# A two-layer block on one core: four of a block's sixteen pair adds given to GpSimd

## The chip, the core and the metric

The kernel runs on one core of a Trainium2 chip. The core has a matrix engine (TensorE, "PE" in the profile, with its weight loads as "PEld"), three elementwise engines (VectorE "DVE", ScalarE "ACT", GpSimd "POOL") and a queue engine for transfers (SyncE "SP"). Each engine works through its own instructions in program order, and engines wait for one another through semaphores. The metric is the device time of one execution in microseconds. Before the change, three runs gave 5608.47, 5620.06 and 5624.56 us; the median is 5620.06.

## What is computed

The reference is two transformer-like layers on x of shape (4, 1024, 256), float32. The first has a recurrence over time and a mixture of experts. The second, which the change touches, has a pairwise attention and a dense feed-forward network:

```python
q = einsum('bnc,ac->bna', X, Wq)          # a = 64
k = einsum('bnc,ac->bna', X, Wk)
Vy = einsum('bnc,dc->bnd', X, Wy_w) + Wy_b
e = relu(rho_signed_sqrt(q[:, :, None, :] + k[:, None, :, :]))
scores = einsum('bija,a->bij', e, Wphi)
ex = exp(scores - max(scores, axis=-1))
denom = sum(ex, axis=-1)
part1 = einsum('bij,bjc->bic', ex, Vy)
Ew = einsum('bij,bija->bia', ex, e)
part2 = einsum('bia,ca->bic', Ew, We_w) + We_b * denom
return (part1 + part2) / (denom + EPS_DEN)
```

For every query i, key j and channel a, q + k is formed, cut at zero, its root is taken (with 1e-8 under it), weighted with Wphi and summed over a for the scores, and weighted with ex and summed over j for Ew. That is 4 x 1024 x 1024 x 64 elements.

## The kernel before

`first_layer` (L143) does the first layer, `pair_attention` (L801) the second one, with the last part of the first layer and the dense network (`dense`, L1196) woven into it.

In the attention a `Block` is 32 queries of one batch; there are 128. It is worked in 8 **pairs**, numbered p from 0 to 7. A pair is one tile `s` of 128 partitions x 2 x 1024 float32. A partition holds one of 16 queries and one of 8 channels; the two **halves** (h = 0 and 1) are two groups of channels, and pairs 0 to 3 and 4 to 7 are the two sets of 16 queries. The keys lie ready in SBUF, repeated over partitions (`kB`), and the queries are a column per partition (`qt`). `Block.pair` (L1305) makes a pair:

- an **add** for each half: key plus query, cut at zero. On ScalarE this is an activation with the query as its bias (L1313), on VectorE a two-step instruction with scalar operands, add and maximum (L1315). The tuple `RELU_ON_SCALAR` (L35) lists by 2p + h which halves ScalarE takes: 0, 2, 4, 8, 10, 12, that is half 0 of pairs 0, 1, 2, 4, 5 and 6. VectorE makes the other ten;
- a **square root** over both halves on ScalarE, in place (L1316);
- the **score matmuls** on TensorE, 8 for each half (L1320), summed over the block in the PSUM tile `sc`.

When a block's scores are there, `top` (L1328) takes the maximum of a row on VectorE (L1330, L1332) with a small matmul (L1333), `exps` (L1335) takes its negative on VectorE (L1337) and the exponentials on ScalarE (L1339), for which ScalarE loads another table, and `spread` (L1342) repeats them over partitions with matmuls into the PSUM tile `xb` (L1345). `turn` and `turned` (L1348 to L1357) transpose them. Then `weigh` (L1359) multiplies each half with `xb` on VectorE, in place, and sums over keys into a column of `ew` (L1364, two instructions in the profile for each half).

The order is written out by hand, and every engine keeps it. The loop from L1463 goes through the blocks and their pairs: weigh pair p of this block; at p = 5 `top` of the next block, at p = 6 its `exps` and first `spread`; then `work(ROOM[p])` (L1429), which issues some of the waiting dense, finishing and preparing steps, with a budget for each p; then `make()` (L1443), which makes the pair that lies 12 ahead (11 in the first blocks). So after the weigh of pair p, pair p + 4 of the next block is made for p up to 3, and pair p - 4 of the block after for p from 4. The tiles `s` come from a ring of 12 buffers (L31): the pair just made uses the buffer that the weigh before it gives free.

A dense step's matmuls go into one of two PSUM banks; two steps later VectorE empties it (L1238, L1213, L1207, L1277). `finish` (L1368) ends four blocks: VectorE computes `fin` (L1410), GpSimd adds it to the input (L1412) and SP stores that (L1413). GpSimd's only other regular work in this stage is the sum at L1278 at the end of a dense tile, also stored by SP. GpSimd issues no transfers here. `prepare` (L918) makes keys, queries and values of the next batch, with transfers on SP (L955, L980).

Of the kernel before, what the change touches and what calls it, by code (L numbers as in the profile page):

```python
# [9 lines left out]
ALU = mybir.AluOpType  # L10
# [21 lines left out]
PREP = 12  # L32
ROOM = (3, 5, 6, 6, 6, 3, 2, 6)
LATE = 2
RELU_ON_SCALAR = (0, 2, 4, 8, 10, 12)  # L35

CONSTS = {"ident": P, "tri": P, "ones": P, "avg": P, "center": P, "heads": P, "gather": P, "rank": NE, "same": P, "pick": 8 * P, "part": 4, "query": 16, "row0": P}
CH_MX, CH_MW, CH_MK, CH_MV, CH_MR, CH_MG, CH_TD, CH_U, CH_LW, CH_LB = range(10)
# [763 lines left out]
def pair_attention(tc, a, link, out, cols_of, seen, ident, eps):  # L802
# [10 lines left out]
    nc = tc.nc  # L813
# [4 lines left out]
    with tc.tile_pool(name="at_w", bufs=1) as wp, tc.tile_pool(name="at_2", bufs=2) as p2, tc.tile_pool(  # L818
# [24 lines left out]
        for i in range(2):  # L843
            t = wp.tile([P, 4, P], F32, tag=f"ewt{i}", name=f"ewt{i}")
            nc.gpsimd.memset(t, 0.0)
            ewt.append(t)
            t = wp.tile([P, 4, 64], F32, tag=f"ew{i}", name=f"ew{i}")
# [34 lines left out]
        kB = {}  # L882
# [415 lines left out]
        class Block:  # L1298
# [6 lines left out]
            def pair(self, p):  # L1305
                t = ring.tile([P, 2, T], F32, tag="s", name="s")
                self.s[p] = t
                s = p // 4
                for h in range(2):
                    g = (2 * p + h) % 8  # L1310
                    q = qtab[self.b][:, 2 * (self.n % NB) + s, g : g + 1]
                    if 2 * p + h in RELU_ON_SCALAR:
                        nc.scalar.activation(t[:, h, :], kB[self.b][g], AF.Relu, bias=q)  # L1313
                    else:
                        nc.vector.tensor_scalar(t[:, h, :], kB[self.b][g], q, 0.0, ALU.add, ALU.max)  # L1315
                nc.scalar.activation(t, t, AF.Sqrt, bias=eps_rho)  # L1316
                for h in range(2):
                    g = (2 * p + h) % 8
                    for j in range(4):
                        nc.tensor.matmul(  # L1320
                            self.sc[32 * j : 32 * j + 32, 0:256],
                            wsel[:, g, 16 * (1 - s) : 16 * (1 - s) + 32],
                            t[:, h, 256 * j : 256 * (j + 1)],
                            start=p == 0 and h == 0,
                            stop=p == 7 and h == 1,
                        )
# [264 lines left out]
```

## Time and profile before

| | us |
|---|---|
| median of 3 runs | 5620.06 (5608.47 to 5624.56) |
| the profiled execution | 5612.39 |
| its span, first to last instruction | 5610.4 |
| first layer and start of the attention | 0 to about 1270 |
| pair attention with dense work | about 1270 to 5390 |
| dense work alone | about 5390 to 5610 |

| busy us, whole span | TensorE | weight loads | VectorE | ScalarE | GpSimd |
|---|---|---|---|---|---|
| | 4574.4 | 2695.6 | 4532.2 | 3854.0 | 534.3 |

TensorE's mean granted clock was 0.884 of full speed. A row of the groups reads: source line, engine, operation, what it writes and what it reads with their shapes, count, then busy time and the mean duration in ns of one, then the idle time of the engine just before these instructions and what ended most of it. A row in the order of time reads: start in us, length in us, engine, line, operation, tiles, number of instructions, and in brackets the idle time before and what ended it. Durations of neighbours on an engine overlap at the ends, so their spacing is somewhat less than their length. The chain of work is followed back from the last instruction, at each step to what released it or to the instruction before it on its engine.

### The profile page before, as it was taken

The numbers are of one execution on the slowest core, as the hardware profiler recorded it, in microseconds if no ns is written. First come the engines' busy times: TensorE is split into PE (matmuls) and PEld (weight loads), VectorE is DVE, ScalarE is ACT, GpSimd is POOL, SyncE is SP. The second block draws the span as 40 slices with busy tenths as digits, with TensorE's granted clock in tenths as the row PEclk, the third lists the DMA queues.
The fourth block names the chain that finished last, engine by engine and source line by source line (L and its number), as shares of the span: only waits on it lengthen the run. The fifth ranks groups of instructions, "written<-read, shape, count | busy, mean of one in ns | idle before, by whom it ended". The sixth has DMA issues, their size and how long they took to land.

```text
span 5610.4 us, 74442 instructions
## 1 busy us (share of the span) xinstructions
PE 4574.4 (82%) x28714; PEld 2695.6 (48%) x28714; DVE 4532.2 (81%) x7889; ACT 3854.0 (69%) x3550; POOL 534.3 (10%) x463
## 2 busy tenths in 40 slices
PE   6789888765778778888896788897888897888888
PEld 2233333332345445555463555564555564555566
DVE  5777777656888888889988788888889989898951
ACT  2322222117888888888887888888788888888840
POOL 3434433220000000000000000000000000000000
PEclk8789999886889889998898889898899898988999
DMA  4333333332011131211112221111211211111123
GB/s 133 100 94 94 95 89 97 102 95 68 25 36 47 38 70 61 82 61 57 45 69 46 60 82 59 51 63 34 71 53 60 87 65 44 57 56 50 44 95 115
DMA packets 223734, 385.48 MB, mean 69 GB/s; under 512 B 69346, under 2 KB 114963, under 8 KB 222995
## 3 DMA queue, kind: packets, MB, share of 16 engines
q1 hardware_dynamic: 211890, 378.46, 21.7%
q8 instruction: 226, 3.70, 0.3%
q10 hardware_dynamic: 11488, 2.25, 0.2%
q14 instruction: 130, 1.06, 0.1%
HBM read 340.74 MB, written 39.86 MB: 68 GB/s over the span
## 4 chain that ended last, share of the span: by engine, by line
PE 44%; DVE 31%; ACT 16%; SPq 4%; issue 3%; DMA 2%; POOL 0%; ACTq 0%; DVEq 0%; POOLq 0%
PE ff_ps L1249 14%; DVE s L1364 13%; PE sc L1320 8%; ACT s L1316 7%; DVE s L1315 5%; PE e_ps L591 5%; PE xb L1345 4%; DVE state L777 2%; ACT s L1313 2%; PE ff_ps L1226 2%; PE out_ps L1268 2%; ACT wide L1290 2%; ACT L1316 2%; DVE pr L779 2%; SPq L955 1%
## 5 line engine op out<-in xcount | busy, mean ns | idle before, releaser
L1364 DVE CUSTOM_DVE_ANT_0 s<-s,xb 128x1024 f32<-128x1024 f32 x2048 | 2412.6, 1215 | 37.7 <-PE xb L1345 36.5
L1316 ACT ACTIVATE s<-s,eps 128x2048 f32<-128x2048 f32 x1024 | 2039.0, 2001 | 379.3 <-DVE s L1315 362.3
L1320 PE MATMUL sc<-s,wsel 128*32 128x256 f32 x16384 | 1235.4, 427 | 727.2 <-ACT s L1316 725.8
L1320 PEld LDWEIGHTS sc<-s,wsel 128*32 128x32 f32 x16384 | 463.3, 117 | 1334.5 <-ACT s L1316 898.6
L1249 PE MATMUL ff_ps<-wide,fw 128*128 128x256 f32 x4096 | 983.5, 389 | 8.6 <-ACT wide L1290 8.5
L1315 DVE TENSOR_SCALAR s<-kB,qt 128x1024 f32<-128x1024 f32 x1280 | 947.3, 758 | 35.3 <-DMA wk<-in_Wk_dram 17.1
L1313 ACT ACTIVATE s<-kB,qt 128x1024 f32<-128x1024 f32 x768 | 875.0, 1139 | 102.7 <-DMA wk<-in_Wk_dram 59.1
L1249 PEld LDWEIGHTS ff_ps<-wide,fw 128*128 128x128 f32 x4096 | 769.2, 193 | 181.9 <-issue 74.5
L1345 PE MATMUL xb<-ex,pick 128*128 128x256 f32 x2048 | 591.6, 439 | 16.6 <-ACT ex L1339 15.8
L1345 PEld LDWEIGHTS xb<-ex,pick 128*128 128x128 f32 x2048 | 423.3, 218 | 208.1 <-issue 75.5
L591 PE MATMUL e_ps<-wd,hid 128*128 128x512 f32 x896 | 424.7, 621 | 0.0
L709 POOL TENSOR_TENSOR kv<-vb,out_k 128x512 f32<-128x512 f32 x256 | 323.7, 1272 | 332.4 <-DVE state L777 202.7
L777 DVE TENSOR_TENSOR_SCAN state<-dec,carry,kv 128x512 f32<-128x512 f32 x256 | 326.0, 1273 | 9.6 <-POOL carry L772 5.0
L1412 POOL TENSOR_TENSOR xr<-xr,fin 128x256 f32<-128x256 f32 x32 | 34.2, 1068 | 2877.8 <-DVE fin L1410 2650.4
L591 PEld LDWEIGHTS e_ps<-wd,hid 128*128 128x128 f32 x896 | 174.8, 201 | 245.0 <-issue 238.4
L779 DVE TENSOR_TENSOR pr<-state,rec 128x512 f32<-128x512 f32 x256 | 176.0, 687 | 110.8 <-ACT state L775 57.5
L1226 PE MATMUL ff_ps<-wide,fw 128*128 128x256 f32 x1024 | 255.5, 400 | 3.3 <-DVE wide L1213 1.5
L1238 DVE TENSOR_TENSOR wide<-ff_ps,ffn_s 128x512 f32<-128x512 f32 x128 | 88.1, 688 | 208.7 <-PE ff_ps L1249 207.7
L769 ACT COPY carry<-state 128x1 f32<-128x1 f32 x255 | 47.8, 188 | 271.4 <-DVE state L777 270.3
L1226 PEld LDWEIGHTS ff_ps<-wide,fw 128*128 128x128 f32 x1024 | 200.2, 201 | 50.1 <-issue 12.1
L1330 DVE TENSOR_REDUCE own<-sc 128x1 f32<-128x256 f32 x128 | 54.0, 422 | 170.6 <-PE sc L1320 170.6
L1364 DVE DVE_READ_ACCUMULATOR2_ANT ew<- 128x1 f32 x2048 | 168.7, 82 | 0.0
(247 smaller groups left out, 3879.9 us busy)
## 6 DMA issues: line engine op xcount, KB each, us to landing
fw<-in_ffw_dram SPq DMA_DIRECT2D x352, 512.0 KB
vb<-vd SPq DMA_DIRECT2D x1024, 64.0 KB
wd<-in_w_down_dram SPq DMA_DIRECT2D x28, 1024.0 KB
kB<-kd SPq DMA_DIRECT2D x32, 512.0 KB
kd<-wide SPq DMA_DIRECT2D x24, 512.0 KB
vd<-out_v SPq DMA_DIRECT2D x8, 512.0 KB
kd<-kn SPq DMA_DIRECT2D x16, 256.0 KB
vy<-vd SPq DMA_DIRECT2D x4, 1024.0 KB
```

Source lines behind the costliest of these rows:

```text
L591: nc.tensor.matmul(ps, hid[:, k, t * P : (t + 1) * P], wd[:, k, :], start=k == 0, stop=k == HID // P - 1)
L709: nc.gpsimd.tensor_mul(kv, vb[:, g % 2, :], ready[u]["k"][:, n // HN, :])
L777: nc.vector.tensor_tensor_scan(s[:, 1 : U + 1], dec, kv, c, ALU.mult, ALU.add)
L779: nc.vector.tensor_mul(pr, s[:, 0:U], rec)
L1226: nc.tensor.matmul(ps[:, h, :], w[:, k, o : o + P], hT[:, k, :], start=k == 0, stop=k == 1)
L1249: nc.tensor.matmul(ps[:, h, :], w[:, k * P : (k + 1) * P], of[:, k, :], start=k == 0, stop=k == 7)
L1313: nc.scalar.activation(t[:, h, :], kB[self.b][g], AF.Relu, bias=q)
L1315: nc.vector.tensor_scalar(t[:, h, :], kB[self.b][g], q, 0.0, ALU.add, ALU.max)
L1316: nc.scalar.activation(t, t, AF.Sqrt, bias=eps_rho)
L1320: nc.tensor.matmul(self.sc[32 * j : 32 * j + 32, 0:256], wsel[:, g, 16 * (1 - s) : 16 * (1 - s) + 32], t[:, h, 256 * j : 256 * (j + 1)], s ...
L1345: nc.tensor.matmul(xb[:, 256 * j : 256 * (j + 1)], pick[:, j, s, :], self.ex, start=True, stop=True)
L1364: nc.vector.tensor_tensor_reduce(t[:, h, :], t[:, h, :], self.xb[s], 1.0, 0.0, ALU.mult, ALU.add, ew[:, self.n % 4, col : col + 1])
```

## The change

GpSimd takes four of a block's adds, `ADD_ON_POOL`: half 1 of pairs 0, 2, 4 and 6. ScalarE's list becomes half 0 of pairs 0, 1, 3, 5 and 7. VectorE keeps seven: half 1 of pairs 1, 3, 5 and 7 and half 0 of pairs 2, 4 and 6. The two halves of a pair are now issued with half 1 first, so that GpSimd's add stands before the other engine's in the program.

```diff
-RELU_ON_SCALAR = (0, 2, 4, 8, 10, 12)
+RELU_ON_SCALAR = (0, 2, 6, 10, 14)
+ADD_ON_POOL = (1, 5, 9, 13)
...
                 s = p // 4
-                for h in range(2):
+                for h in (1, 0):
                     g = (2 * p + h) % 8
                     q = qtab[self.b][:, 2 * (self.n % NB) + s, g : g + 1]
-                    if 2 * p + h in RELU_ON_SCALAR:
+                    if 2 * p + h in ADD_ON_POOL:
+                        nc.gpsimd.tensor_scalar(t[:, h, :], kB[self.b][g], q, 0.0, ALU.add, ALU.max)
+                    elif 2 * p + h in RELU_ON_SCALAR:
                         nc.scalar.activation(t[:, h, :], kB[self.b][g], AF.Relu, bias=q)
                     else:
                         nc.vector.tensor_scalar(t[:, h, :], kB[self.b][g], q, 0.0, ALU.add, ALU.max)
```

## The prediction

> **What bounds the kernel now.** I read the busy times first, then one stretch of the second layer, then the chain of work that ended last, then the groups, and last the order of time around single instructions.
>
> ```profile
> PE 4574.4 (82%) x28714; PEld 2695.6 (48%) x28714; DVE 4532.2 (81%) x7889; ACT 3854.0 (69%) x3550; POOL 534.3 (10%) x463
> 4650.00:5150.00 500.00, 425.65 (x3204) 274.13 (x3197) 448.86 (x792) 439.07 (x324) 7.71 (x6) 0.90 0.15 52
> PE 44%; DVE 31%; ACT 16%; SPq 4%; issue 3%; DMA 2%; POOL 0%; ACTq 0%; DVEq 0%; POOLq 0%
> ```
>
> The second line is a stretch inside the pair attention (TensorE, weight loads, VectorE, ScalarE, GpSimd). VectorE is busy 90% of it, ScalarE 88%, TensorE 85%, GpSimd under 2%. So three engines are nearly full and coupled, and none is the bound alone; the third line, the chain's shares, says the same. An edit there is worth its count on the chain, not its busy time.
>
> ```profile
> L1364 DVE CUSTOM_DVE_ANT_0 s<-s,xb 128x1024 f32<-128x1024 f32 x2048 | 2412.6, 1215 | 37.7 <-PE xb L1345 36.5
> L1316 ACT ACTIVATE s<-s,eps 128x2048 f32<-128x2048 f32 x1024 | 2039.0, 2001 | 379.3 <-DVE s L1315 362.3
> L1315 DVE TENSOR_SCALAR s<-kB,qt 128x1024 f32<-128x1024 f32 x1280 | 947.3, 758 | 35.3 <-DMA wk<-in_Wk_dram 17.1
> L1313 ACT ACTIVATE s<-kB,qt 128x1024 f32<-128x1024 f32 x768 | 875.0, 1139 | 102.7 <-DMA wk<-in_Wk_dram 59.1
> L410 POOL TENSOR_TENSOR rk<-out_r,out_k 128x1024 f32<-128x1024 f32 x8 | 18.8, 2348 | 3.1 <-ACT out_r L403 3.1
> L845 POOL MEMSET ewt<- 128x512 f32 x2 | 1.1, 526 | 1.9 <-DMA x<-x 1.9
> ```
>
> Durations overlap at their ends, so I cost by the spacing of starts in the order of time: an add on VectorE 0.67 us, a weigh 1.14 (two with what follows: 2.40), a square root on ScalarE 1.91, an add there 1.17. A pair with one add on each engine takes VectorE 3.07 and ScalarE 3.08 us.
>
> From 1650 to 5376 us (115 of 128 blocks) I went through the chain in order of time and gave each add and square root the pair it belongs to, by its running number. Square roots on the chain: pair 1 61 times, pair 2 62, pair 7 14, pair 6 11, the others 3 to 7. 49 times the chain goes from VectorE's add of pair 1 into its square root, on through the exponentials on ScalarE, and out by pair 2's add and square root to TensorE. VectorE's adds on it: pair 0 69, pair 7 first half 54, pair 3 first half 25; the second halves of pairs 2, 4, 6: 25, 29, 35. ScalarE's: pair 2 62, pair 6 12, pair 4 3.
>
> **The change, part by part.** Of a block's adds, half 1 of pairs 0, 2, 4, 6 goes from VectorE to GpSimd; half 0 of pairs 2, 4, 6 goes from ScalarE to VectorE; half 0 of pairs 3 and 7 from VectorE to ScalarE. No DMA, tile or matmul changes.
>
> *Saved on ScalarE:* pair 2's add leaves a run in which ScalarE alone is on the chain: 62 x 1.14 = 71 us; pairs 4 and 6: 15 x 1.14 = 17; the new adds lengthen pairs 3 and 7, whose square roots are on the chain 5 + 14 times: 19 x 1.14 = 22 lost. Net 66.
>
> *Saved on VectorE:* pairs 3 and 7: 79 x 0.67 = 53. Pair 0 would be 69 x 0.67 = 46, but behind 49 of these ScalarE has a path almost as long: from the end of the weigh, 0.04 + 1.17 + 1.91 + 1.17 = 4.29 us to pair 1's square root, against VectorE's 0.67 + 2.40 + 0.60 (the row maximum) + 0.75 = 4.42. So 49 x 0.13 + 20 x 0.67 = 19. Pairs 2, 4, 6 swap one add for another: 0. **Saved in all: 66 + 53 + 19 = 138 us.**
>
> *The length of the GpSimd add* is not in the trace. Its product of two tensors takes 0.73 us for 256 elements, 1.27 for 512 and 2.35 for 1024 (2.1 ns an element), its memset of 512 0.53 (0.84 ns an element between 256 and 512; 0.96 us for 1024 as an estimate). An add with one tensor input lies between. The Trainium skill ("GPSIMD Engine Reference", section 4.1 Engine selection) says not to put elementwise work there, and calls one-input operations roughly line-rate; its section 3.1 gives a best loop of about 1.8 cycles an element at 1.2 GHz. The estimates by it are 1.05 and 1.7 us with the 0.18 us of start that the trace's rows leave. I take **1.65**, the middle of the trace's two rows, and keep 1.0 to 2.35, and more if its loop is poor.
>
> *The port.* Here a rule speaks against the change:
>
> ```profile
> 1915.28 1.28 POOL L1278 TENSOR_TENSOR res<-res,wide 128x512 f32<-128x512 f32 x1 [42.86 <-DVE wide L1277]
> 2250.67 2.42 DVE L1315 TENSOR_SCALAR s<-kB,qt 128x1024 f32<-128x1024 f32 x2
> 2250.98 1.57 POOL L1278 TENSOR_TENSOR res<-res,wide 128x512 f32<-128x512 f32 x1 [109.61 <-issue]
> 3035.32 0.74 DVE L1315 TENSOR_SCALAR s<-kB,qt 128x1024 f32<-128x1024 f32 x1
> 3035.49 1.17 POOL L1412 TENSOR_TENSOR xr<-xr,fin 128x256 f32<-128x256 f32 x1 [59.75 <-DVE fin L1410]
> 3035.98 1.21 DVE L1364 CUSTOM_DVE_ANT_0 s<-s,xb 128x1024 f32<-128x1024 f32 x1
> ```
>
> Two VectorE adds take 1.41 us alone; with a GpSimd sum started inside the first they take 2.42. The sum waited for the first add and the second add waited 1.01 us for the sum, whose own length is 1.28. The weigh (one operand in PSUM) runs beside GpSimd unhurt. The Trainium skill ("SBUF — State Buffer", Who interferes with whom) says that whoever issues first holds the shared pair for the whole instruction. By the rule a VectorE add behind a 1.65 us add waits up to 1.65, by the row 1.65 - 0.27 = 1.38; I use the row. Who is first?
>
> ```profile
> 4698.25 0.08 DVE L1364 DVE_READ_ACCUMULATOR2_ANT ew<- 128x1 f32 x1
> 4698.37 1.15 ACT L1313 ACTIVATE s<-kB,qt 128x1024 f32<-128x1024 f32 x1 [0.28 <-DVE ew L1364]
> 4698.37 0.75 DVE L1315 TENSOR_SCALAR s<-kB,qt 128x1024 f32<-128x1024 f32 x1
> ```
>
> The ring has 12 buffers and runs 12 ahead, so a pair's adds wait for the weigh just issued. VectorE's add starts 0.04 us after it, ScalarE's too; GpSimd starts 0.08 to 0.09 us after the VectorE result it waits for (L1410 ends at 3035.40, L1412 starts at 3035.49). So being earlier in the program does not help GpSimd: I take VectorE first, by 0.04 us. Of the 345 adds of pairs 2, 4, 6, 230 follow the weigh at once; in 29 GpSimd is held by the sum of L1412 anyway; in 86 other VectorE work stands between and GpSimd gets the port. Summed over their gaps, that stalls VectorE 31 us (10 for an add of 1.25 us, 81 for 2.35).
>
> *The new wait.* A square root of pair 2, 4 or 6 can start 0.04 + 0.67 + 1.65 + 0.04 = 2.40 us after the weigh, that of pair 0 (no VectorE add) at 1.77; now both start at 1.22 where ScalarE has no backlog. Behind it on ScalarE are the next pair's add, exponentials and copies; on TensorE its score matmuls, and behind those the dense layers. Pair 2 is free of it: its square root starts no earlier than 3.95 now. Costs on the chain: pair 0 before the 49 crossings, 49 x 0.55 = 27; pairs 4 and 6, 14 x 1.2 = 17; the backlog that pair 6 hands through pair 7 to pair 0, 0.65 us at about half of the 49, 16; the port, 31 us at the share of adds on the chain (0.35), 11; the row maximum and the weigh, which wait for TensorE 32 and 43 times now, about 0.4 us later each, 30. **Cost: 101 us.** On GpSimd's queue a block adds 4 x 1.65 = 6.6 us to an engine idle 98% here; the sums of L1412 and L1278, and their stores on SP's queue, come at most one add later.
>
> **Sum.** -138 + 101 = -37 us in 115 blocks, x 128/115 = -41. The profiled execution took 5612.4 us (span 5610.4, 2.0 around it): 5571. It lies 7.7 under the median of the runs, 5620.1: **5580 us**, 0.7% less. The last 221 us, dense layers alone, and the first layer stay.
>
> **The rivals.** *A short GpSimd add, 1.05 us:* the costs fall to 0 + 8 + 3 + 1 + 10 = 22, net -116 x 1.11 = -129: **5490**. For it the memset row; against it the two-tensor row. Were the three adds a block saved in full, 384 x 0.67 = 257, it would be 5363, but VectorE is under a third of the chain.
>
> *GpSimd gets the port first (slower):* at the 230 adds that follow the weigh at once VectorE waits 1.38 + 0.04 = 1.42, 327 us; 89 of 345 of them are on the chain, 84 us, less 10 as those square roots come earlier: -37 + 84 - 10 = +37, x 1.11 = 41: **5661**. It decides when the claim comes under 0.04 us after the weigh. Against it the 0.08 us; for it that both are tens of nanoseconds.
>
> *A long GpSimd add, 2.35 us:* 61 + 27 + 16 + 28 + 60 = 192, less 138 = +54, x 1.11 = 60: **5680**; at 3 us some 5780. Between 1.65 and 2.35 the balance turns at about 1.93.
>
> **How the numbers follow.** The sum's case 0.47 (own range 5545 to 5615), short add 0.13, port 0.15, long add 0.25. 0.3% (17 us) is about what a measurement of this kernel can tell. Sum's case: 0.33 faster, 0.10 same, 0.04 slower; short: 0.13 faster; port: 0.02 same, 0.13 slower; long: slower. Faster 0.46, same 0.12, slower 0.42. The range, 5480 to 5720, leaves out the ends of the short and long cases.
>
> **What would show it.** 512 GpSimd TENSOR_SCALARs of 128x1024; their length undisturbed (pair 0) is the first number to read: 1.65 holds the sum, over 1.93 breaks it. In pairs 4 and 6 GpSimd's records stretch by about 0.6 us (waiting for VectorE) while VectorE's adds stay near 0.75; adds of 2 us there mean that GpSimd was first. ScalarE's wait of L1316 moves from VectorE to GpSimd, mostly in pairs 0, 4, 6. VectorE busy falls by some 250 us, ScalarE by 146. Wrong I would also be if TensorE's granted clock, 0.90 here, fell with denser work.

## The result

The changed kernel took 5748.92 us (median of 4 runs, 5747.30 to 5754.26) against 5614.62 before on the same chip: 1.0238 times as long, 95% interval 1.0222 to 1.0255. I had forecast 5580, with a range up to 5720. It is 134 us slower, and 29 us above the range.

The profile after, in the order of the lines shown for before. First the busy times of the whole span, and the same stretch of 500 us (TensorE, weight loads, VectorE, ScalarE, GpSimd):

```profile
PE 4614.3 (80%) x28714; PEld 2695.9 (47%) x28714; DVE 4331.8 (75%) x7505; ACT 3710.6 (65%) x3422; POOL 2569.0 (45%) x975
4650.00:5150.00 500.00, 411.63 (x3108) 262.31 (x3107) 411.25 (x725) 411.51 (x301) 255.16 (x69) 0.90 0.15 50
```

VectorE lost 200 us of work (250 were forecast) and ScalarE 143 (146), as the change intends. In the stretch VectorE is busy 82% (90% before), ScalarE 82% (88%), TensorE 82% (85%). All three have less to do per unit of time and the kernel is longer: work was replaced by waiting. Then the groups:

```profile
L1314 POOL TENSOR_SCALAR s<-kB,qt 128x1024 f32<-128x1024 f32 x512 | 2038.2, 3981 | 1871.6 <-DVE ew L1367 1282.6
L1319 ACT ACTIVATE s<-s,eps 128x2048 f32<-128x2048 f32 x1024 | 2049.3, 2002 | 705.1 <-POOL s L1314 655.7
L1318 DVE TENSOR_SCALAR s<-kB,qt 128x1024 f32<-128x1024 f32 x896 | 719.9, 804 | 32.0 <-DMA wk<-in_Wk_dram 16.9
L1367 DVE CUSTOM_DVE_ANT_0 s<-s,xb 128x1024 f32<-128x1024 f32 x2048 | 2403.8, 1213 | 130.8 <-PE xb L1348 117.1
L1333 DVE TENSOR_REDUCE own<-sc 128x1 f32<-128x256 f32 x128 | 54.2, 423 | 427.6 <-PE sc L1323 427.3
```

(The square root is now L1319, the weigh L1367, VectorE's add L1318.) GpSimd's add takes 3.98 us on average, 3.70 undisturbed. ScalarE's square root waits 656 us for it. What follows from a late root is seen on VectorE, which waits for the score matmuls of a block before the row maximum: 428 us, against 171 before the change and 236 in the kernel that leaves GpSimd's adds out (`e_none`, below). The wait before the weigh, 131 us (38 before), must not be put down to late roots: it is 115 us in `e_none` too, where no root waits for GpSimd. The rows of before, then of `e_none`:

```profile
L1330 DVE TENSOR_REDUCE own<-sc 128x1 f32<-128x256 f32 x128 | 54.0, 422 | 170.6 <-PE sc L1320 170.6
...
L1371 DVE CUSTOM_DVE_ANT_0 s<-s,xb 128x1024 f32<-128x1024 f32 x2048 | 2405.9, 1215 | 115.2 <-PE xb L1352 113.3 <-ACT wide L1291 1.6
L1337 DVE TENSOR_REDUCE own<-sc 128x1 f32<-128x256 f32 x128 | 54.1, 423 | 235.9 <-PE sc L1327 235.9
```

Last, in the order of time, pair 6 of a block: the weigh's end, VectorE's add, GpSimd's add, VectorE's next add and the root that waited.

```profile
4805.09 0.08 DVE L1367 DVE_READ_ACCUMULATOR2_ANT ew<- 128x1 f32 x1
4805.21 0.75 DVE L1318 TENSOR_SCALAR s<-kB,qt 128x1024 f32<-128x1024 f32 x1
4805.36 4.16 POOL L1314 TENSOR_SCALAR s<-kB,qt 128x1024 f32<-128x1024 f32 x1 [3.05 <-DVE ew L1367]
...
4808.76 1.31 DVE L1318 TENSOR_SCALAR s<-kB,qt 128x1024 f32<-128x1024 f32 x1
4809.56 2.00 ACT L1319 ACTIVATE s<-s,eps 128x2048 f32<-128x2048 f32 x1 [2.13 <-POOL s L1314]
```

VectorE is first at the port, 0.15 us ahead, and GpSimd's add is stretched from 3.70 to 4.16 us by it. It then lasts so long that VectorE's add of the next pair runs into it (1.31 us instead of 0.75). The root starts 4.39 us after the weigh's end (4805.17).

### The profile page after: what moved, and what is told of

The parts are those of the page before. It is cut to its first block, busy times and chain, and to the rows that moved or that the text cites. A ratio compares the mean times of both kernels' runs of the same rounds, so it can differ in the third digit from the quotient of the medians.

```text
span 5748.4 us, 75177 instructions
## 1 busy us (share of the span) xinstructions
PE 4614.3 (80%) x28714; PEld 2695.9 (47%) x28714; DVE 4331.8 (75%) x7505; ACT 3710.6 (65%) x3422; POOL 2569.0 (45%) x975
## 3 DMA queue, kind: packets, MB, share of 16 engines
q14 instruction: 135, 1.11, 0.1%
## 5 line engine op out<-in xcount | busy, mean ns | idle before, releaser
L1314 POOL TENSOR_SCALAR s<-kB,qt 128x1024 f32<-128x1024 f32 x512 | 2038.2, 3981 | 1871.6 <-DVE ew L1367 1282.6
L1319 ACT ACTIVATE s<-s,eps 128x2048 f32<-128x2048 f32 x1024 | 2049.3, 2002 | 705.1 <-POOL s L1314 655.7
L1367 DVE CUSTOM_DVE_ANT_0 s<-s,xb 128x1024 f32<-128x1024 f32 x2048 | 2403.8, 1213 | 130.8 <-PE xb L1348 117.1
L1323 PE MATMUL sc<-s,wsel 128*32 128x256 f32 x16384 | 1266.9, 434 | 832.0 <-ACT s L1319 785.0
L1316 ACT ACTIVATE s<-kB,qt 128x1024 f32<-128x1024 f32 x640 | 727.6, 1137 | 61.5 <-DMA wk<-in_Wk_dram 58.6
L1318 DVE TENSOR_SCALAR s<-kB,qt 128x1024 f32<-128x1024 f32 x896 | 719.9, 804 | 32.0 <-DMA wk<-in_Wk_dram 16.9
```

What stands on the lines that cost most here:

```text
L1314: nc.gpsimd.tensor_scalar(t[:, h, :], kB[self.b][g], q, 0.0, ALU.add, ALU.max)
L1323: nc.tensor.matmul(self.sc[32 * j : 32 * j + 32, 0:256], wsel[:, g, 16 * (1 - s) : 16 * (1 - s) + 32], t[:, h, 256 * j : 256 * (j + 1)], s ...
L1367: nc.vector.tensor_tensor_reduce(t[:, h, :], t[:, h, :], self.xb[s], 1.0, 0.0, ALU.mult, ALU.add, ew[:, self.n % 4, col : col + 1])
```

## The experiments

Four numbers have to be told apart: the instruction's own length, the port, the late root, and the new split of adds between VectorE and ScalarE. All times are medians, set against runs of the kernel before on the same chip (5620 to 5628 us).

**GpSimd's instructions alone** (`forms`), a kernel of nothing but these.

> GpSimd alone, no VectorE beside it: five each of the add used here (two steps, query column as scalar) over 1024, 512 and 256 elements, the same with a constant instead of the column, with one step and the column, with one step and a constant, a copy, a sum of two tensors and a memset, 1024 elements each. The kernel computes nothing else; its output is only the input. Theory 'the instruction itself is long': the two-step add takes about 3.7 us here as well, with a slope of about 3.5 ns an element. Rival 'the port makes it long': here it takes 1.0 to 2.35 us as the prediction had it, and the 3.7 us came from VectorE. One step should lie clearly under two steps if the cost is the arithmetic, and equal if it is the loop.

The groups of that kernel, tile names after the form, mean ns after the comma:

```profile
L32 POOL TENSOR_SCALAR two<-x,q 128x1024 f32<-128x1024 f32 x5 | 18.5, 3708 | 9.3 <-DMA x<-in_x_dram 9.3
L35 POOL TENSOR_SCALAR twoimm<-x 128x1024 f32<-128x1024 f32 x5 | 18.2, 3640 | 0.0
L38 POOL TENSOR_SCALAR oneptr<-x,q 128x1024 f32<-128x1024 f32 x5 | 14.4, 2871 | 0.0
L41 POOL TENSOR_SCALAR oneimm<-x 128x1024 f32<-128x1024 f32 x5 | 14.0, 2793 | 0.0
L47 POOL TENSOR_TENSOR added<-x 128x1024 f32<-128x1024 f32 x5 | 11.8, 2370 | 0.0
L32 POOL TENSOR_SCALAR two<-x,q 128x512 f32<-128x512 f32 x5 | 10.0, 2000 | 0.0
L44 POOL COPY copied<-x 128x1024 f32<-128x1024 f32 x5 | 5.3, 1067 | 0.0
L50 POOL MEMSET wiped<- 128x1024 f32 x5 | 4.8, 952 | 0.5 <-POOLq L60 0.3
```

With no VectorE beside it the add takes 3.71 us, so the port does not make it long. From 512 to 1024 elements it grows by 1.71 us, 3.3 ns an element. A part of it is the arithmetic: one step is 2.87, a second step adds 0.84. A tensor_scalar instruction with one step takes longer than the sum of two tensors (2.37), and a copy, also one tensor input, is near the memset.

**The GpSimd adds left out** (`e_none`).

```diff
                     if 2 * p + h in ADD_ON_POOL:
-                        nc.gpsimd.tensor_scalar(t[:, h, :], kB[self.b][g], q, 0.0, ALU.add, ALU.max)
+                        continue
...
-                nc.scalar.activation(t, t, AF.Sqrt, bias=eps_rho)
+                if 2 * p + 1 in ADD_ON_POOL:
+                    keys = kB[self.b][(2 * p + 1) % 8].unsqueeze(1).to_broadcast([P, 2, T])
+                    nc.scalar.activation(t, keys, AF.Sqrt, bias=eps_far)
+                else:
+                    nc.scalar.activation(t, t, AF.Sqrt, bias=eps_rho)
```

(`eps_far` is a new column that holds 400.)

> The changed kernel with GpSimd's four adds left out (the square root of those pairs reads the keys instead, in the same size, and still waits for the other half's add through its output tile). So that part of the computation is missing. The saving on VectorE and ScalarE is there, the GpSimd wait is not. Prediction's sum without its costs: 138 us x 1.11 less than before, about 5460 us. Theory 'late square root': 5440 to 5520. Rival 'the new split between VectorE and ScalarE is itself bad' (an add moved to ScalarE in pairs 3 and 7): 5600 or more.

5431.5 us, 0.9659 of before (0.9643 to 0.9676): 196 us less, more than I had expected. The split and the relief are good; what spoils them is GpSimd.

**The port without the wait** (`e_beside`).

```diff
                     if 2 * p + h in ADD_ON_POOL:
-                        nc.gpsimd.tensor_scalar(t[:, h, :], kB[self.b][g], q, 0.0, ALU.add, ALU.max)
+                        if self.n > 1:
+                            m, pw = divmod(8 * self.n + p - RING, 8)
+                            col = 32 * (pw // 4) + (2 * pw + 1) % 8
+                            pace = ews[m // 4 % 2][:, m % 4, col : col + 1]
+                            nc.gpsimd.tensor_scalar(beside, kB[self.b][g][:, 0:BESIDE], pace, 0.0, ALU.add, ALU.max)
```

(`BESIDE` is 864. The root of these pairs is as in the kernel above. To make room for the tile `beside`, the tiles `s3`, `fin` and `xr` have one buffer each instead of two; what that costs alone was not tried.)

> As the kernel without GpSimd adds, but GpSimd makes an add of 864 keys into a tile that nobody reads, started by the same weigh as before (its scalar is the column that the weigh writes). So the port is held as in the changed kernel for about 0.85 of the time, and no square root waits; those adds are missing from the result. Theory 'late square root': within 50 us of the kernel without GpSimd adds (VectorE adds that meet GpSimd cost about 40 us at most). Rival 'the shared port': close to the changed kernel, 5700 or more.

5463.4 us, 0.9715 (0.9698 to 0.9731), 32 us over the kernel without GpSimd adds. The groups of this kernel between 1300 and 5600 us, GpSimd's and VectorE's add:

```profile
L1320 POOL TENSOR_SCALAR beside<-kB,ew 128x864 f32<-128x864 f32 x504 | 1719.8, 3412 | 1885.0 <-DVE ew L1377 1504.8
...
L1324 DVE TENSOR_SCALAR s<-kB,qt 128x1024 f32<-128x1024 f32 x889 | 753.5, 848 | 15.1
```

VectorE's add is 848 ns on average here, 750 without GpSimd: 98 ns x 896 = 88 us lost at the port, of which at most 32 reach the end. In the changed kernel these adds are shorter, 804 ns, so the port takes no more from VectorE there. It is real and small; the wait of the root is the rest, about 290 us (5463 to 5750). In that rest is also what GpSimd's add loses to the add of VectorE that is ahead of it, 4.16 us instead of 3.70 in pairs 4 and 6; that part was not separated.

**The order of the halves** (`e_order`): `for h in (1, 0)` back to `for h in range(2)`.

> The changed kernel with half 0 issued before half 1, as before the change. Each engine's own order stays, apart from half 0 and half 1 never lying on the same engine in a pair. Both theories: the same as the changed kernel within 10 us, since GpSimd starts when the weigh ends, not when it is issued.

5750.4 us, 1.0223 (1.0200 to 1.0246), as the changed kernel. Issuing GpSimd first does nothing.

**A shorter instruction in its place** (`e_len1`, `e_len2`): the wait stays, the instruction is another one, and the adds are missing from the result.

```diff
-                        nc.gpsimd.tensor_scalar(t[:, h, :], kB[self.b][g], q, 0.0, ALU.add, ALU.max)
+                        nc.gpsimd.memset(t[:, h, :], 0.5)                          # e_len1
+                        nc.gpsimd.tensor_mul(t[:, h, :], kB[self.b][g], kB[self.b][g])   # e_len2
```

> The changed kernel with GpSimd writing a constant (memset, 0.95 us for 1024 elements) where it made the add, so those adds are missing; every wait stays, the length falls from 3.70 to 0.95 us. Theory 'only the length was wrong': the prediction's own working for a short add, 1.05 us, applies: 129 us less than before, about 5500; as the kernel without GpSimd adds gained 196 rather than 153, down to 5440 is in it. Rival 'any wait of the square root on GpSimd costs': 5580 or more.

> As the kernel with a memset, but GpSimd multiplies the keys with themselves (two tensor inputs, 2.37 us for 1024 elements); the adds are missing. Theory 'the length decides, in proportion': the prediction gave +60 us for 2.35 us; between the measured ends (196 less without GpSimd, some 130 more at 3.7 us) a straight line gives about 10 more, and a threshold at the slack of the square root gives less: 5520 to 5690. Rival 'port': the same as the kernel with the tile beside, about 5460.

5516.4 us (0.9816, 0.9795 to 0.9837), 105 less than before, and 5575.9 us (0.9915, 0.9898 to 0.9931), 46 less. The product of a tensor with itself was shorter than the 2.37 us of two different tensors that I had put in (shortest, median and longest duration in ns after the colon):

```profile
L1314 POOL TENSOR_TENSOR s<-kB x512: 1884/1896/2408, 1293.8 to 5337.0; 128x1024 f32<-128x1024 f32 x171
```

So the changed kernel with instructions of 0.95, 1.90 and 3.70 us is 105 and 46 faster and 134 slower. Between the last two the balance turns, on a straight line, at 1.90 + 1.80 x 46 / 180 = 2.4 us (an estimate). The rival "any wait on GpSimd costs" fell: both are faster than before.

The memset, though, changed more than the length. It starts 0.11 us after VectorE's add, and that add then lasts 1.61 us instead of 0.75; so it is in 214 of the 216 places where VectorE's add follows the weigh at once (from the thirteenth block on). In the changed kernel it is in none of 189. The memset, pair 6 of a block, and then VectorE's adds between 1300 and 5600 us:

```profile
4004.77 1.61 DVE L1318 TENSOR_SCALAR s<-kB,qt 128x1024 f32<-128x1024 f32 x1
4004.88 0.95 POOL L1314 MEMSET s<- 128x1024 f32 x1 [6.03 <-ACT s L1319]
4006.47 2.00 ACT L1319 ACTIVATE s<-s,eps 128x2048 f32<-128x2048 f32 x1 [1.58 <-DVE s L1318]
...
L1318 DVE TENSOR_SCALAR s<-kB,qt 128x1024 f32<-128x1024 f32 x889 | 866.3, 975 | 15.1
```

Against the kernel without GpSimd adds `e_len1` is still 91 us slower, while its roots wait only 58.5 us for GpSimd. VectorE's longer adds, about 0.22 x 896 = 200 us of work, are the likelier cost here. The point at 0.95 us is therefore none of length alone. At 1.90 us the means of VectorE's adds are closer, 844 ns against 804 in the changed kernel.

**One pair alone** (`v_pair2`, `v_pair2s`, `e_pair6s`):

```diff
-RELU_ON_SCALAR = (0, 2, 6, 10, 14)
-ADD_ON_POOL = (1, 5, 9, 13)
+RELU_ON_SCALAR, ADD_ON_POOL = (0, 2, 4, 8, 10, 12), (5,)    # v_pair2
+RELU_ON_SCALAR, ADD_ON_POOL = (0, 2, 8, 10, 12), (5,)       # v_pair2s
+RELU_ON_SCALAR, ADD_ON_POOL = (0, 2, 4, 8, 10), (13,)       # e_pair6s
```

> The kernel before with one add more on GpSimd: half 1 of pair 2 alone, taken from VectorE; ScalarE's list as before. Pair 2 follows the exponentials on ScalarE, its square root starts no earlier than 3.95 us after the weigh, and GpSimd is done 0.19 + 3.70 = 3.89 us after it. Theory 'a late square root costs, a hidden one does not': faster than before, by 25 chain adds x 0.67 = 17 us up to 60. Rival 'port': GpSimd then holds the port when VectorE wants it next, the same or slower.

5625.2 us, 1.0006 (0.9996 to 1.0015): no gain, and my theory missed. The root of pair 2 is not late (4.68 us after the weigh at the median, 4.62 before). But GpSimd still holds the port when VectorE comes to pair 3, which has two adds there. One case, 2.22 us for two adds that take 1.41 alone:

```profile
4539.63 3.70 POOL L1314 TENSOR_SCALAR s<-kB,qt 128x1024 f32<-128x1024 f32 x1 [29.59 <-DVE neg L1340]
4542.31 2.22 DVE L1318 TENSOR_SCALAR s<-kB,qt 128x1024 f32<-128x1024 f32 x2
```

In 87 of 116 blocks one of the two is longer than 0.85 us, each time with GpSimd's add still under way; on average they take 0.97 against 0.75, so 232 x 0.22 = 51 us are lost of the 128 x 0.67 = 86 that VectorE was spared. Here the port rival was right.

> As the kernel with pair 2's half 1 on GpSimd, but half 0 of pair 2 goes from ScalarE to VectorE, so VectorE keeps ten adds and ScalarE makes five. This takes the add that stands most often on the chain (62 times 1.14 us); GpSimd then often waits for VectorE's add and is done 0.04 + 0.67 + 3.7 = 4.4 us after the weigh, where the square root could start at 2.8 without its ScalarE add. Theory: gains where the root starts late anyway (median 4.62), little elsewhere: 5560 to 5620. Rival 'ScalarE's load does not matter': as before.

> The same trade as in the kernel with pair 2 on GpSimd and VectorE, but at pair 6 (half 1 to GpSimd, half 0 from ScalarE to VectorE), whose square root can start 1.2 us after the weigh now (median 1.66). GpSimd is done 4.4 us after it. Theory 'what counts is how late the root of that pair could start anyway': no gain or slower, 5610 to 5690. Rival 'any pair does, the load counts': about 5550 as at pair 2.

The same trade is 70 us faster at pair 2 (5551.6, 0.9874, 0.9856 to 0.9892) and 90 us slower at pair 6 (5710.4, 1.0160, 1.0144 to 1.0175). Both lie outside what I had expected, on either side. At pair 6 the root starts 4.39 us after the weigh at the median, 1.66 before; at pair 2 4.78 against 4.62. The roots of all pairs wait for GpSimd 394.5 us in the kernel with pair 6 and 68.7 in the one with pair 2 (between 1650 and 5500 us); the row of the first:

```profile
ACT s L1319 <- POOL s L1314: 394.5, 113, 5.8
```

So the place decides, not the load. But the place counts twice: for the wait, and for what ScalarE's relief is worth, as the next kernel shows.

**ScalarE's share of that gain** (`e_act2`): `RELU_ON_SCALAR = (0, 2, 8, 10, 12)`, `ADD_ON_POOL = ()`. No GpSimd; against the kernel before, one add a block goes from ScalarE to VectorE.

> No add on GpSimd; the kernel before with half 0 of pair 2 moved from ScalarE to VectorE (eleven adds there, five on ScalarE). It splits the gain of the kernel with pair 2 on GpSimd and VectorE (70 us) into the part from ScalarE's relief and the part from GpSimd. Theory 'ScalarE's add of pair 2 stands on the chain 62 times': 71 us saved less 128 x 0.67 x 0.35 = 30 for the added VectorE work: about 5580. Rival 'the gain is GpSimd's': 5620 or more.

5521.1 us, 0.9824 (0.9807 to 0.9840): 99 us less than before, and the best of the kernels that leave nothing out. I had expected 40. Giving pair 2's other half to GpSimd on top, as `v_pair2s` does, costs 30 us. The gain at pair 2 is thus ScalarE's relief, and GpSimd took from it; the split alone at pair 6 was not run, so what GpSimd's half costs there is open. VectorE has one add a block more than before and yet waits less for the weigh's other operand (12.6 us; 37.7 before). What else makes up the 99 us was not followed. The groups of this kernel between 1300 and 5600 us:

```profile
L1367 DVE CUSTOM_DVE_ANT_0 s<-s,xb 128x1024 f32<-128x1024 f32 x2048 | 2413.2, 1217 | 12.6 <-PE xb L1348 12.1
...
L1318 DVE TENSOR_SCALAR s<-kB,qt 128x1024 f32<-128x1024 f32 x1397 | 1026.2, 758 | 18.2
```

**Roots issued later** (`v_defer`, `v_defer4`): the root and score matmuls of a pair with a GpSimd add are issued behind those of the next pair. (`v_defer` has `ADD_ON_POOL = (1, 5, 9)`: pair 6 is back on VectorE.)

```diff
+                if p in ROOT_LATER:          # (0, 4); v_defer4: (0, 4, 6)
+                    self.held.append(p)
+                    return
+                self.root(p)
+                while self.held:
+                    self.root(self.held.pop())
```

> GpSimd makes half 1 of pairs 0, 2 and 4; the square roots and score matmuls of pairs 0 and 4 are issued one pair later, behind those of pairs 1 and 5, so ScalarE and TensorE have work while GpSimd is busy; pair 2 follows the exponentials. Pair 6 goes back to VectorE (both halves), eight adds there, five on ScalarE. Theory 'late root': most of the gain without GpSimd's wait (196 us) less one VectorE add a block: 5450 to 5540. Rival 'the port or GpSimd's share in itself': 5580 or more.

> As the kernel with late roots for pairs 0 and 4, with all four adds of the change on GpSimd and the root of pair 6 issued behind that of pair 7 as well. It differs from the changed kernel by the order of roots alone. Theory: 5450 to 5560, unless the last root (pair 6, about 5 us after pair 7's weigh, scores 1.1 later, while the row maximum comes 5.5 us after it) makes the row maximum wait, some 0.5 us a block. Rival 'port': 5700 or more as the changed kernel.

5636.5 us (1.0037, 1.0023 to 1.0051) and 5674.5 us (1.0095, 1.0077 to 1.0112). `v_defer4` differs from the changed kernel by the order of roots alone and is 76 us better, but both missed my numbers. In `v_defer` the root waits only 13 us for GpSimd, as intended. But the root of pair 0 now stands between that of pair 1 and the exponentials, and VectorE waits for the weigh's other operand 182 us (131 in the changed kernel, 115 in `e_none`; `v_defer`, same groups):

```profile
L1330 ACT ACTIVATE s<-s,eps 128x2048 f32<-128x2048 f32 x1023 | 2009.7, 1997 | 310.4 <-DVE s L1320 285.9 <-POOL s L1316 13.1
L1379 DVE CUSTOM_DVE_ANT_0 s<-s,xb 128x1024 f32<-128x1024 f32 x2048 | 2405.7, 1216 | 181.8 <-PE xb L1360 175.9
```

A part of the delay was moved to another wait. The exponentials end 7.9 us after the weigh of pair 5 at the median, against 6.7 in `e_none` and 5.8 before. That this order is the cause is argued from these figures; I did not run a kernel that defers pair 4 alone.

**The split without GpSimd** (`e_nopool`), the change's list for ScalarE and `ADD_ON_POOL = ()`, and **one add less on ScalarE** (`v_act4`), `RELU_ON_SCALAR = (0, 2, 8, 10)`, no GpSimd.

> The changed kernel with the four adds of GpSimd on VectorE: ScalarE has half 0 of pairs 0, 1, 3, 5 and 7, VectorE the other eleven. Theory 'ScalarE's relief before the exponentials is most of the saving': 5500 to 5560, so that the four adds on VectorE are worth about 70 to 130 us (from there to 5431 without GpSimd). Rival 'VectorE's load is the saving, as half of the prediction's sum had it': 5600 or more.

> No add on GpSimd; ScalarE keeps half 0 of pairs 0, 1, 4 and 5, VectorE makes twelve (the kernel with pair 2's add on VectorE, and pair 6's moved too). Theory 'pair 2 was the special place': no further gain, 5510 to 5560, since pair 6's add stood on the chain 12 times only and VectorE gets 86 us more. Rival 'ScalarE's load as such': another 50 us or more below 5521.

5557.3 us (0.9884, 0.9866 to 0.9903), 65 less than before, and 5565.6 us (0.9896, 0.9877 to 0.9916), 57 less. Relieving ScalarE at pair 6 too gives 42 of the 99 us back, which is more than I had expected: pair 2 was the special place.

Together they lead from before to after:

| step | us against before | difference |
|---|---|---|
| the new split, all other adds on VectorE | -65 | -65 |
| GpSimd's four adds off VectorE, nobody makes them | -196 | -131 |
| GpSimd holds the port (864 keys), nobody waits | -165 | +32 |
| the root waits for 3.70 us | +122 to +134 | about +290 |

## Why the prediction was wrong

**What bounds the kernel: held.** Taking four adds a block off VectorE, 512 x 0.67 = 343 us of work, gave about 130 us, 38%; the count of VectorE's adds on the chain had said 35%. Counting on the chain was right to the size here.

**The savings: right in sign, too small.** The sum had 138 x 1.11 = 153 us; with GpSimd's adds gone it was 196. The undersized term is ScalarE's add of pair 2: I gave it 71 us from 62 places on the chain, 79 over all blocks; moving it alone brought 99 although VectorE had to take it over. That an earlier root of pair 2 also spares waits that the chain of before didn't pass is likely, not shown.

**The length of the GpSimd add: this is the step that failed.** The sum had 1.65 us, and 3.70 was measured. "An add with one tensor input lies between" the memset and the two-tensor product took the number of tensors read for what costs time on that engine, and it is false: the add lies far over the 2.35 that I took for the far end. "And more if its loop is poor" stood in the text, but the high end of the range was made from 2.35. The Trainium skill's "roughly line-rate" for one-input operations ("GPSIMD Engine Reference", section 4.1 Engine selection) fits the copy (1.07 us) and not this instruction; the measurement decides. The trace of before had no tensor_scalar on GpSimd, so no row was near, and a bound from other kinds of instruction was none.

**The port: held.** VectorE was first, as worked out, where its add follows the weigh at once: none of 189 such adds of pairs 2, 4 and 6 took over 0.85 us. Where other VectorE work stands between, 57 of 159 did. GpSimd's records start 0.19 us after the weigh, where I had 0.08. In the changed kernel VectorE's adds are 804 ns instead of 750 on average, 896 x 0.054 = 48 us, some of it at a place I had not looked at: the add of the next pair, 3 us later (0.88 us on average in pair 5), which a 1.65 us instruction would not have reached.

**The wait: right mechanism, sized for another length.** The root of pairs 4 and 6 was to start at 0.04 + 0.67 + L + 0.04 after the weigh; with L = 3.70 that is 4.45. Measured at the median were 4.39 in pair 6 and 4.78 in pair 4. ScalarE's idle time before roots went over to GpSimd in pairs 0, 4 and 6 as written (103, 296 and 172 of 605 us in the last 116 blocks). The prices can be set against the kernel without GpSimd adds. At 1.90 us the terms give about 148 us over all blocks, and 196 - 46 = 150 were measured; that no gain was forecast there came from the savings. At 3.70 us, with the slope that the terms have between 1.65 and 2.35, they give about 410 (an estimate), and 196 + 134 = 330 were measured. That they add up delays that overlap is likely, not shown.

**The clock.** The last sign of being wrong, a fall of TensorE's granted clock, does not carry the result. In the stretch it is 0.90 before and after. Over the whole span it went from 0.884 to 0.875, and the same 28714 matmuls were busy for 40 us more, which bounds its part of the 134 us. Whether the clock fell because TensorE waited more is open.

**The rivals.** The third, a long GpSimd add, is what happened, with a chance of 0.25. The second, GpSimd first at the adds that follow the weigh at once, did not.

## What to carry to other kernels

Before work goes to an idle engine, get the length of that very instruction there; a bound from other instructions of the engine is no bound. If the consumer waits for it, compare that length with how late the consumer could start anyway, pair by pair: roots waited 69 us for GpSimd where the root was late and 394 where it was early. And among nearly full, coupled engines look first for the instruction that stands on the chain most often: moving pair 2's add from ScalarE to the busiest engine gained more than any use of the idle one.

## What the runs showed of the hardware that I had not expected

- GpSimd's tensor_scalar over 128x1024 float32 takes 2.79 us with one step and a constant, 2.87 with a column, 3.64 and 3.71 with two steps; a sum of two tensors 2.37, a product of a tensor with itself 1.90, a copy 1.07, a memset 0.95.
- A GpSimd add starts 0.19 us after the weigh that it waits for, VectorE's and ScalarE's 0.04. A long GpSimd instruction also hits VectorE's adds of the next pair: in `v_pair2` 51 us were lost in pair 3 to an add of pair 2.
- A memset on GpSimd held up a VectorE add that had started 0.11 us before it: 1.61 us instead of 0.75 in 214 of 216 places of `e_len1`. GpSimd's own add, started 0.15 us after VectorE's, waited instead (4.16 us instead of 3.70) and left VectorE's at 0.75. So the rule that the first to issue keeps the port, which the prediction took, did not hold for the memset.
